# The second layer of a four-layer network: one matrix for each gate, chunks of 1024 columns in a fixed order

## The chip, the cores and the metric

The kernel runs on one core of a Trainium2 chip. The metric is the device time of one execution in microseconds (us); lower is better. The engines are named as in the profile: PE (TensorE, its weight loads apart as PEld), DVE (VectorE), ACT (ScalarE), POOL (GpSimd) and SP (SyncE, which here only issues DMAs). A "q" after a name (ACTq, SPq) is the engine's queue where it issues DMAs or waits.

## The reference

Four layers follow each other on a tensor of 8 images, 16 channels and 128 x 128 pixels in float32. Each adds its result to its input. The change is in the second (the code calls it layer 1), between a normalization over pairs of channels and the sum with the input:

```python
x = x + _L1_conv_ref(_gn(x), Wc, bc, W1, b1, W2, b2, W3, b3, W4, b4)

def _L1_conv_ref(x, Wc, bc, W1, b1, W2, b2, W3, b3, W4, b4):
    out1 = jnp.mean(x, axis=(2, 3), keepdims=True)
    out3 = jnp.max(x, axis=(2, 3), keepdims=True)
    out2 = conv1x1(x, Wc, bc)
    out4 = conv1x1(x, W1, b1)
    wh = conv1x1(out2 / (out1 + EPS), W2, b2)
    wh_weight = sigmoid(tanh(wh))
    gray = conv1x1(out4 / (out3 + EPS), W3, b3)
    gray_weight = sigmoid(tanh(gray))
    return conv1x1(x * (1.0 + wh_weight + gray_weight), W4, b4)
```

Each conv1x1 is a 16 x 16 matrix on the channels of a pixel plus a bias. Between the two convolutions of a gate there is only a factor for each image and channel, from the mean or the maximum of the image. The layers around it (an attention block on 3 x 3 windows, rational functions, splines) are not touched.

## The kernel before

The 8 images times 16 channels lie on the 128 partitions; a row holds the 16384 pixels of an image's channel. The layers run one after another. The first leaves its result in DRAM and the statistics of it in SBUF; the second reads it into a tile x (line 758), which stays in SBUF and is updated in place by the second and third layer.

The weights of the second layer are loaded at the very start of the kernel (lines 218 to 226). Each of the five 16 x 16 matrices becomes a block diagonal 128 x 128 tile w1s[n], by a memset on POOL and eight DMAs issued by ACT (line 224), each followed by eight small DMAs that repeat a bias (rep, line 172). Other DMAs of ACT stand before and behind these. ACT takes its instructions in order, so its first activation, the square root of the first normalization (line 197, recorded as line 152), comes behind these issues. SP loads the input (line 240) at the same time, and DVE takes its statistics.

The second layer itself begins with weight work for the third and fourth layer: SP loads parts of the weights, DVE spreads them (line 784, 36 operations), multiplies and sums splines (lines 810, 812, 820, 814, 823). This work has no place written out; the scheduler lays it among the rest. Then come the normalization's mean and rs (group_stats, lines 178 to 206, which ends in rs at line 203), and rmean and rmax, the reciprocals of mean and maximum for each image and channel (lines 833 to 839).

Then 32 chunks of 512 columns (line 841). For each chunk: DVE normalizes x to y (line 844); for each of the two gates PE multiplies with w1s[n] (line 848), DVE adds the bias and multiplies with rmean or rmax (line 850), PE multiplies with w1s[2 + n] (line 852), ACT takes tanh with the bias and then the sigmoid (lut, line 152). DVE adds the two gates and 1 (line 857), POOL multiplies y with that (line 860), PE multiplies with w1s[4] (line 862), DVE adds bias and x (line 863) and takes the statistics of the new x for the next normalization (line 866). The order of the chunks on each engine is left to the scheduler. SBUF tiles of this loop have three buffers, PSUM tiles (p1, p2, p3 of one bank each) two.

The third layer begins when the statistics are complete: group_stats again, then POOL clears eight tiles f (line 909), and DVE, ACT and POOL make powers of x (lines 890 to 901) that go to DRAM and come back before its first product on PE (line 927).

An order is forced where in_turn is used (lines 210 to 215): it ties an instruction behind the one named before it in the same chain, without a wait, so that the scheduler keeps that order on the engine. The first, third and fourth layer use it; the second doesn't. The lut helper ties activations to the table set they need.

Of the kernel before, what the change touches and what calls it, by code (L numbers as in the profile page):

```python
# [9 lines left out]
F32 = mybir.dt.float32  # L10
AF = mybir.ActivationFunctionType
ALU = mybir.AluOpType
AX = mybir.AxisListType
PSUM = bass.MemoryType.PSUM
# [86 lines left out]
def kernel(  # L101
# [43 lines left out]
    def lut(out_, in_, func, **kw):  # L145
        name = sets.get(func, str(func))
        last = phase["all"]
        if name != phase["name"]:
            phase.update(name=name, first=None, all=[])
            if name == "exp_ln":  # L150
                begin(nc.scalar.preload_act_table_set("natural_log_exp_and_others").ins, last)
        ins = nc.scalar.activation(out_, in_, func, **kw).ins  # L152
        if phase["first"] is None:
            begin(ins, last)
        else:
            tc.add_manual_dep(ins, phase["first"].name, order, reason="table set")
        phase["all"].append(ins)
        return ins
# [51 lines left out]
    def in_turn(engine, ins):  # L210

        if engine in chain:
            tc.add_manual_dep(ins, chain[engine].name, order, reason="in turn")
        chain[engine] = ins
        return ins
# [3 lines left out]
    for n in range(5):  # L219
        t = cpool.tile([BC, BC], F32, name=f"w1_{n}")  # L220
        nc.gpsimd.memset(t, 0.0)
        for b in range(B):
            r = slice(b * C, (b + 1) * C)
            nc.scalar.dma_start(t[r, r], w1[n])
        w1s.append(t)
        b1s.append(rep(b1[n], B, f"b1_{n}"))

# [6 lines left out]
    with ExitStack() as l0:  # L234
# [137 lines left out]
        class Variances:  # L372
# [3 lines left out]
            def __init__(self, first, others):  # L376
                self.due = [first + n * others for n in (4, 2, 4, 2)]
                self.begun = [False] * 4

            def add(self, t, c, sq):  # L380
                i = t // 32
                self.due[i] -= 1
                pe(
                    banks[t : t + 32, 0],
                    halfvar[:, 30 - c : 62 - c],
                    sq,
                    start=not self.begun[i],
                    stop=self.due[i] == 0,
                )
                self.begun[i] = True  # L390
# [373 lines left out]
    with ExitStack() as l1:  # L764
        wp = l1.enter_context(tc.tile_pool(name="w1", bufs=1))
        tmp = l1.enter_context(tc.tile_pool(name="tmp1", bufs=3))

        wa = rational.tile([128, 2, 9, 4, C], F32, name="wa")
        wb = rational.tile([128, 2, 9, 4, C], F32, name="wb")
        chan = k_("chan").unsqueeze(2).to_broadcast([128, 4, C])
        for t, src, least in ((wa, a2, 0), (wb, q2, 1)):
            for s in range(2):
                dense = wp.tile([128, 144], F32, name="dense", bufs=2)
                nc.gpsimd.memset(dense, 0.0)
                for u in range(4):
                    for i in range(1, src.shape[0] // C + least):  # L780
                        lo, r = 32 * (u ^ s) + 4 * (i - 1), C * (i - least) + 4 * u
                        nc.sync.dma_start(dense[lo : lo + 4], src[r : r + 4])
                for n in range(9):
                    nc.vector.tensor_tensor(
                        t[:, s, n],
                        dense[:, n * C : (n + 1) * C].unsqueeze(1).to_broadcast([128, 4, C]),
                        chan,
                        ALU.mult,
                    )
        for s in range(2):  # L790
            for u in range(4):
# [12 lines left out]
        nc.sync.dma_start(w, w3_spline)  # L804
        sc = wp.tile([128, 144, 9], F32, name="sc")
        bs = wp.tile([BC, 144, 9], F32, name="bs")
        for i in range(8):
            nc.sync.dma_start(sc[i * C : (i + 1) * C], w3_scaler)
            nc.scalar.dma_start(bs[i * C : (i + 1) * C], w3_base)
        nc.vector.tensor_mul(w, w, sc)  # L810
        red = wp.tile([128, 9, C], F32, name="red")
        nc.vector.tensor_reduce(red.rearrange("p n f -> p (n f)"), w, AX.X, ALU.add)
        redb = wp.tile([BC, 9, C], F32, name="redb")
        nc.vector.tensor_reduce(redb.rearrange("p n f -> p (n f)"), bs, AX.X, ALU.add)
        for s in range(4):
            for p in range(2):
                if 0 <= s - p < 3:
                    n = slice(3 * (s - p), 3 * (s - p) + 3)

                    nc.vector.tensor_scalar_mul(wspl[:, s, :, p, :], red[:, n], -1.0 / 6.0)  # L820
                    rows = slice(32 * s, 32 * s + 32)
                    for g in range(2):
                        nc.vector.tensor_scalar_mul(
                            wbase[rows, g, :, p, :],
                            redb[rows, n],
                            k_("image")[rows, 2 * s + g : 2 * s + g + 1],
                        )

        mean, dm, rs, _ = group_stats(bn1, "1")
        xmax = wp.tile([BC, 1], F32, name="xmax")  # L830
        nc.vector.tensor_reduce(xmax, top, AX.X, ALU.max)

        rmean = wp.tile([BC, 1], F32, name="rmean")
        nc.vector.tensor_scalar(rmean, dm, rs, EPS, ALU.mult, ALU.add)
        nc.vector.reciprocal(rmean, rmean)
        rmax = wp.tile([BC, 1], F32, name="rmax")
        nc.vector.tensor_scalar(rmax, xmax, mean, rs, ALU.subtract, ALU.mult)
        nc.vector.tensor_scalar_add(rmax, rmax, EPS)
        nc.vector.reciprocal(rmax, rmax)
        ps = l1.enter_context(tc.tile_pool(name="ps1", bufs=2, space=PSUM))  # L840
        for j in range(NCH):
            cols = bass.ts(j, 512)
            y = tmp.tile([BC, 512], F32, name="y1")
            nc.vector.tensor_scalar(y, x[:, cols], mean, rs, ALU.subtract, ALU.mult)
            gates = []
            for n, r in ((0, rmean), (1, rmax)):
                p1 = ps.tile([BC, 512], F32, name="p1")
                mm(p1, w1s[n], y, start=True, stop=True)
                t1 = tmp.tile([BC, 512], F32, name="t1")
                nc.vector.tensor_scalar(t1, p1, b1s[n], r, ALU.add, ALU.mult)  # L850
                p2 = ps.tile([BC, 512], F32, name="p2")
                mm(p2, w1s[2 + n], t1, start=True, stop=True)
                gt = tmp.tile([BC, 512], F32, name=f"gate{n}")
                lut(gt, p2, AF.Tanh, bias=b1s[2 + n])
                lut(gt, gt, AF.Sigmoid)
                gates.append(gt)
            nc.vector.scalar_tensor_tensor(
                gates[0], gates[0], 1.0, gates[1], op0=ALU.add, op1=ALU.add
            )
            nc.gpsimd.tensor_mul(y, y, gates[0])  # L860
            p3 = ps.tile([BC, 512], F32, name="p3")
            mm(p3, w1s[4], y, start=True, stop=True)
            nc.vector.scalar_tensor_tensor(
                x[:, cols], p3, b1s[4], x[:, cols], op0=ALU.add, op1=ALU.add
            )
            nc.vector.bn_stats(bn2[:, j], x[:, cols])


    bn3 = cpool.tile([BC, NCH, 6], F32, name="bn3")
    with ExitStack() as l2:  # L870
# [51 lines left out]
        def product(p, w, g, k, n, q):  # L922

            dh, dw = divmod(n, 3)
            for u in range(4):
                lo = 32 * (u ^ (q % 2))
                yield mm(  # L927
                    p[64 * (u % 2) : 64 * (u % 2) + 64, u // 2],
                    w[lo : lo + 32, q % 2, n].rearrange("p c f -> p (c f)"),
                    fs[g * NP + q][lo : lo + 32, 4 * k + dh : 4 * k + dh + 4, dw : dw + W],  # L930
                    start=True,
                    stop=True,
                ).ins
# [488 lines left out]
```

## Time and profile before

| What | us |
|---|---|
| median of 3 runs (lowest to highest) | 11350.83 (11344.36 to 11351.51) |
| the profiled execution, whole | 11347.98 |
| its span in the profile | 11345.9 |
| the second layer's first product on PE starts (line 848) | 3431.5 |
| its last product ends (line 862) | 3627.1 |
| the third layer's first product starts (line 927) | 3659.3 |
| the fourth layer's first activation (line 1105) | 10667.3 |

The span begins with the first instruction of the profile and ends with its last; the execution's time is 2.1 us longer. The second layer has less than 2% of the span; the third has more than 60%. In the lists of groups, a line gives the source line, engine, operation, what is written from what, the number of instructions, then after the bar the busy time in us and the mean of one in ns, and after the second bar the idle time of the engine just before these instructions, with what ended it.

### The profile page before, as it was taken

The numbers are of one execution on the slowest core, as the hardware profiler recorded it, in microseconds if no ns is written. First come the engines' busy times: TensorE is split into PE (matmuls) and PEld (weight loads), VectorE is DVE, ScalarE is ACT, GpSimd is POOL, SyncE is SP. The second block draws the span as 40 slices with busy tenths as digits, with TensorE's granted clock in tenths as the row PEclk, the third lists the DMA queues.
The fourth block names the chain that finished last, engine by engine and source line by source line (L and its number), as shares of the span: only waits on it lengthen the run. The fifth ranks groups of instructions, "written<-read, shape, count | busy, mean of one in ns | idle before, by whom it ended". The sixth has DMA issues, their size and how long they took to land.

```text
span 11345.9 us, 174363 instructions
## 1 busy us (share of the span) xinstructions
PE 8924.7 (79%) x72492; PEld 2115.6 (19%) x72492; DVE 9125.6 (80%) x6935; ACT 8792.4 (77%) x7187; POOL 4870.3 (43%) x2697
## 2 busy tenths in 40 slices
PE   5999999999986777777777777777777777777788
PEld 1222222222222111111111111111111111111122
DVE  3555555555555699999999999999999999999865
ACT  2555555555543699999999999999999999999876
POOL 3556555565542743333333334343343334344300
PEclk8999999999998799999999999999999999999999
DMA  1000000000002300000000000000000000000022
GB/s 48 12 15 15 15 12 13 15 15 14 13 6 67 130 20 7 7 13 7 7 13 7 7 13 7 7 13 7 7 10 10 7 7 13 7 7 7 20 53 50
DMA packets 185552, 203.94 MB, mean 18 GB/s; under 512 B 42936, under 2 KB 151608, under 8 KB 182712
## 3 DMA queue, kind: packets, MB, share of 16 engines
q1 hardware_dynamic: 180264, 190.81, 6.3%
q8 instruction: 570, 9.34, 0.3%
q10 hardware_dynamic: 4496, 1.97, 0.1%
q14 instruction: 222, 1.82, 0.1%
HBM read 107.15 MB, written 60.04 MB: 15 GB/s over the span
## 4 chain that ended last, share of the span: by engine, by line
DVE 44%; PE 31%; ACT 14%; issue 5%; POOL 2%; DMA 1%; SPq 1%; DVEq 0%; ACTq 0%; POOLq 0%
DVE t L959 22%; PE banks L360 17%; DVE u L965 14%; PE pn L927 10%; ACT t L948 8%; DVE y L518 2%; PE acc L1278 2%; POOL y L527 1%; DVE x L538 1%; ACT u L152 1%; PE pd L927 1%; ACT hid L152 1%; SPq L1242 1%; DMA yd<-y 1%; DVE x L630 1%
## 5 line engine op out<-in xcount | busy, mean ns | idle before, releaser
L927 PE MATMUL pn<-f,wa 32*64 32x512 f32 x18432 | 3424.1, 626 | 1706.7 <-DVE u L965 1672.7
L980 POOL TENSOR_TENSOR v<-t,u 128x1024 f32<-128x1024 f32 x1152 | 2738.0, 2377 | 4027.0 <-DVE t L959 3865.8
L965 DVE TENSOR_TENSOR u<-pn,u 128x1024 f32<-128x1024 f32 x2304 | 2715.3, 1220 | 123.6 <-DVE t L959 6.9
L927 PE MATMUL pd<-f,wb 32*64 32x512 f32 x18432 | 2608.4, 628 | 158.4 <-ACT t L948 92.3
L959 DVE SCALAR_TENSOR_TENSOR t<-t,u 128x2048 f32<-128x2048 f32 x1152 | 2631.2, 2284 | 34.4 <-ACT u L152 33.9
L948 ACT ACTIVATE t<-pd 128x1024 f32<-128x1024 f32 x2304 | 2336.7, 1014 | 320.0 <-PE pn L927 312.6
L152 ACT ACTIVATE u<-t 128x2048 f32<-128x2048 f32 x1152 | 2202.5, 1912 | 54.8 <-PE acc L1011 19.1
L152 ACT ACTIVATE u<-u 128x2048 f32<-128x2048 f32 x1152 | 2190.9, 1902 | 0.0
L927 PEld LDWEIGHTS pn<-f,wa 32*64 32x64 f32 x18432 | 752.0, 132 | 3777.2 <-DVE u L965 3243.1
L972 DVE SCALAR_TENSOR_TENSOR u<-t,u 128x1024 f32<-128x1024 f32 x1152 | 1419.1, 1232 | 37.6
L152 ACT ACTIVATE hid<-banks 128x1024 f32<-128x1024 f32 x576 | 571.4, 1023 | 1044.4 <-PE banks L360 1042.6
L1011 PE MATMUL acc<-u,const 128*32 128x512 f32 x9216 | 1263.2, 621 | 1.9 <-DVE u L972 1.9
L527 POOL TENSOR_TENSOR y<-y 128x1536 f32<-128x1536 f32 x256 | 894.6, 3495 | 830.5 <-DVE y L518 830.5
L518 DVE TENSOR_TENSOR y<-banks,vp 128x1536 f32<-128x1536 f32 x384 | 673.2, 1753 | 274.6 <-PE banks L360 271.3
L544 ACT ACTIVATE sq<-x 128x1024 f32<-128x1024 f32 x384 | 397.9, 1054 | 413.4 <-DVE x L538 290.7
L470 POOL TENSOR_TENSOR pd<-q,kp 128x1536 f32<-128x1536 f32 (+1 forms) x256 | 693.4, 2733 | 6.8 <-PE banks L360 6.7
L927 PEld LDWEIGHTS pd<-f,wb 32*64 32x64 f32 x18432 | 515.3, 132 | 753.3 <-ACT t L948 691.0
L360 PE MATMUL banks<-att,const 32*128 32x512 f32 x2304 | 497.4, 668 | 173.9 <-DVE att L509 96.2
L360 PE MATMUL banks<-h,wfc 64*128 64x512 f32 (+1 forms) x3072 | 619.7, 632 | 14.5 <-DVE h L606 14.5
L1011 PE MATMUL acc<-v,const 128*32 128x512 f32 x4608 | 616.8, 606 | 0.2 <-POOL v L980 0.2
L606 DVE TENSOR_TENSOR h<-banks,x 128x1024 f32<-128x1024 f32 x192 | 232.6, 1211 | 435.5 <-ACT hid L152 227.5
L1278 PE MATMUL acc<-s,wspl 128*32 128x512 f32 x3072 | 386.8, 646 | 92.6 <-DVE o L1291 92.6
(177 smaller groups left out, 7501.1 us busy)
## 6 DMA issues: line engine op xcount, KB each, us to landing
f<-yd SPq DMA_DIRECT2D x512, 101.6 KB
yd<-y SPq DMA_DIRECT2D x320, 130.0 KB
xin<-in_x SPq DMA_DIRECT2D x752, 32.0 KB
four<-sil SPq DMA_DIRECT2D x256, 65.0 KB
xj<-in_x SPq DMA_DIRECT2D x8, 1024.0 KB
xl<-in_x SPq DMA_DIRECT2D x32, 256.0 KB
x1d<-xl SPq DMA_DIRECT2D x32, 256.0 KB
x<-x1d SPq DMA_DIRECT2D x8, 1024.0 KB
```

Of the source, the lines that this page charges most:

```text
L152: ins = nc.scalar.activation(out_, in_, func, **kw).ins
L360: in_turn("pe", mm(*args, skip_group_check=True, **kw).ins)
L470: ins = nc.gpsimd.tensor_mul(t[:, :n].rearrange("p n (a b) -> p n a b", a=4), rows(self.q[d][:, k]).unsqueeze(1).to_broadcast([128, n, 4, W]),
L518: ins = nc.vector.tensor_mul(y.rearrange("p n (a b) -> p n a b", a=4), banks[:, 1:4].rearrange("p n (a b) -> p n a b", a=4), windows(v, j, 3),
L527: in_turn("pool", nc.gpsimd.tensor_add(self.y[k], self.y[k], y).ins)
L927: yield mm(p[64 * (u % 2) : 64 * (u % 2) + 64, u // 2], w[lo : lo + 32, q % 2, n].rearrange("p c f -> p (c f)"), fs[g * NP + q][lo : lo + ...
L948: in_turn("act", nc.scalar.activation(self.t[:, ab], self.pd.pop(ab), AF.Abs).ins)
L959: ins = nc.vector.scalar_tensor_tensor(self.t, self.t, 1.0, self.u, op0=ALU.add, op1=ALU.mult).ins
L965: ins = nc.vector.tensor_mul(self.u[:, ab], self.pn.pop(ab), self.u[:, ab]).ins
L972: ins = nc.vector.scalar_tensor_tensor(r, self.t[:, :, 0], 2.0, r, op0=ALU.subtract, op1=ALU.mult).ins
L980: ins = nc.gpsimd.tensor_mul(self.v, self.t[:, :, 1], self.u[:, :, 1]).ins
L1011: ins = mm(accs[k][32 * q : 32 * q + 32], gather[:, int(part == 1), g], (c.u[:, ab, 0], c.u[:, ab, 1], c.v[:, ab])[part], start=first, sto ...
```

## The change

The two convolutions of a gate are made one. With the factor r of the image between them, W2 (r (W1 y + b1)) + b2 is (W2 r W1) y + (W2 r b1 + b2). So after rmean and rmax are known, the kernel scales w1s[2 + n] by r, multiplies the two matrices and the bias on PE, and copies the results to SBUF: a 128 x 128 matrix gates[n] and a column shifts[n] for each gate. For this product the first matrix of each gate is needed the other way round, so line 224 loads w1[0] and w1[1] transposed, by an access pattern on the DRAM side.

The loop then has 16 chunks of 1024 columns. A chunk is an object with steps; each step's instructions on DVE, PE and ACT are put into a chain of that engine with in_turn. One sigmoid covers both gates. Each turn of the loop works on three chunks: the gates of chunk j, the norm of chunk j + 1, the sum of the gates and POOL's multiplication of chunk j - 1, and the last product and update of chunk j - 2. In PSUM the gate products have three buffers of two banks and the last product one of two banks, which is all of it. In SBUF y has five buffers and the gates three. The products of the setup have a PSUM pool of their own that is closed before.

```diff
-            nc.scalar.dma_start(t[r, r], w1[n])
+            nc.scalar.dma_start(t[r, r], w1[n].rearrange("i o -> o i") if n < 2 else w1[n])
...
-        ps = l1.enter_context(tc.tile_pool(name="ps1", bufs=2, space=PSUM))
-        for j in range(NCH):
-            cols = bass.ts(j, 512)
-            y = tmp.tile([BC, 512], F32, name="y1")
-            nc.vector.tensor_scalar(y, x[:, cols], mean, rs, ALU.subtract, ALU.mult)
-            gates = []
+
+        gates, shifts = [], []
+        with tc.tile_pool(name="ps_gate", bufs=2, space=PSUM) as pp:
             for n, r in ((0, rmean), (1, rmax)):
-                p1 = ps.tile([BC, 512], F32, name="p1")
-                mm(p1, w1s[n], y, start=True, stop=True)
-                t1 = tmp.tile([BC, 512], F32, name="t1")
-                nc.vector.tensor_scalar(t1, p1, b1s[n], r, ALU.add, ALU.mult)
...
+                scaled = wp.tile([BC, BC], F32, name=f"scaled{n}")
+                nc.vector.tensor_scalar_mul(scaled, w1s[2 + n], r)
+                pg = pp.tile([BC, BC], F32, name="pg")
+                mm(pg, w1s[n], scaled, start=True, stop=True)
+                ph = pp.tile([BC, 1], F32, name="ph")
+                mm(ph, scaled, b1s[n], start=True, stop=True)
+                gate = wp.tile([BC, BC], F32, name=f"w_gate{n}")
+                nc.vector.tensor_copy(gate, pg)
+                shift = wp.tile([BC, 1], F32, name=f"b_gate{n}")
+                nc.vector.tensor_add(shift, ph, b1s[2 + n])
+                gates.append(gate)
+                shifts.append(shift)
+        ps = l1.enter_context(tc.tile_pool(name="ps1", bufs=3, space=PSUM))
+
+        class Chunk:
+            def __init__(self, j):
+                self.j, self.x = j, x[:, bass.ts(j, 1024)]
+
+            def norm(self):
+                self.y = tmp.tile([BC, 1024], F32, name="y1", bufs=5)
+                ins = nc.vector.tensor_scalar(
+                    self.y, self.x, mean, rs, ALU.subtract, ALU.mult
+                ).ins
+                in_turn("dve1", ins)
+
+            def product(self, p, w):
+                for i in range(2):
+                    cols = bass.ts(i, 512)
+                    in_turn("pe1", mm(p[:, cols], w, self.y[:, cols], start=True, stop=True).ins)
+
+            def gate(self):
+                self.g = tmp.tile([BC, 2, 1024], F32, name="gate")
+                for n in range(2):
+                    p = ps.tile([BC, 1024], F32, name="p_gate")
+                    self.product(p, gates[n])
+                    in_turn("act1", lut(self.g[:, n], p, AF.Tanh, bias=shifts[n]))
+                in_turn("act1", lut(self.g, self.g, AF.Sigmoid))
+
+            def add(self):
+                g = self.g
+                ins = nc.vector.scalar_tensor_tensor(
+                    g[:, 0], g[:, 0], 1.0, g[:, 1], op0=ALU.add, op1=ALU.add
+                ).ins
+                in_turn("dve1", ins)
+                nc.gpsimd.tensor_mul(self.y, self.y, g[:, 0])
+
+            def last(self):
+                self.p = ps.tile([BC, 1024], F32, name="p_last", bufs=1)
+                self.product(self.p, w1s[4])
+
+            def update(self):
+                ins = nc.vector.scalar_tensor_tensor(
+                    self.x, self.p, b1s[4], self.x, op0=ALU.add, op1=ALU.add
+                ).ins
+                in_turn("dve1", ins)
+                for i in range(2):
+                    j = 2 * self.j + i
+                    ins = nc.vector.bn_stats(bn2[:, j], self.x[:, bass.ts(i, 512)]).ins
+                    in_turn("dve1", ins)
+
+        chunks = [Chunk(j) for j in range(HW // 1024)]
+        chunks[0].norm()
+        for j in range(len(chunks) + 2):
+            steps = (("gate", j), ("norm", j + 1), ("add", j - 1), ("last", j - 2), ("update", j - 2))
+            for do, i in steps:
+                if 0 <= i < len(chunks):
+                    getattr(chunks[i], do)()
```

More of the change, by code (lines that the diff above doesn't have):

```diff
@@ L839 @@
         nc.vector.reciprocal(rmax, rmax)
-        ps = l1.enter_context(tc.tile_pool(name="ps1", bufs=2, space=PSUM))
-        for j in range(NCH):
-            cols = bass.ts(j, 512)
-            y = tmp.tile([BC, 512], F32, name="y1")
-            nc.vector.tensor_scalar(y, x[:, cols], mean, rs, ALU.subtract, ALU.mult)
-            gates = []
-            for n, r in ((0, rmean), (1, rmax)):
-                p1 = ps.tile([BC, 512], F32, name="p1")
-                mm(p1, w1s[n], y, start=True, stop=True)
-                t1 = tmp.tile([BC, 512], F32, name="t1")
[L850 to L866, printed above, removed]
```

## The prediction

> **What bounds the kernel now.** I read the page first: which engine is full, and where.
>
> ```profile
> PE 8924.7 (79%) x72492; PEld 2115.6 (19%) x72492; DVE 9125.6 (80%) x6935; ACT 8792.4 (77%) x7187; POOL 4870.3 (43%) x2697
> ```
>
> No engine is full on average, and the average says nothing of the second layer, 198 us of 11346. So the next view is busy time by window: the whole second layer, ten of its chunks in the steady state, and the start of the kernel, which one line of the diff touches.
>
> ```profile
> 3431.00:3629.00 198.00, 154.13 (x320) 60.22 (x320) 136.70 (x239) 84.87 (x131) 43.75 (x37) 0.96 0.07 21
> 3545.00:3601.00 56.00, 45.74 (x102) 18.22 (x101) 39.55 (x61) 25.38 (x41) 12.65 (x10) 1.00 0.00 0
> 0.00:59.00 59.00, 1.17 (x4) 1.00 (x4) 22.00 (x40) 0.35 (x1) 3.83 (x20) 1.00 0.51 161
> ```
>
> The columns are length, then PE, PEld, DVE, ACT and POOL busy, clock, DMA share, GB/s. In the steady state PE is busy 82% and DVE 71%; neither is full, so the order of work leaves holes. Third view: the groups of those 56 us.
>
> ```profile
> L848 PE MATMUL p<-y,w 128*128 128x512 f32 x42 | 19.8, 592 | 0.0
> L852 PE MATMUL p<-t,w 128*128 128x512 f32 x40 | 18.8, 592 | 0.0
> L152 ACT ACTIVATE gate<-p,b 128x512 f32<-128x512 f32 x21 | 14.2, 678 | 30.0 <-PE p L852 30.0
> L860 POOL TENSOR_TENSOR y<-y,gate 128x512 f32<-128x512 f32 x10 | 12.7, 1265 | 43.2 <-DVE gate L857 43.2
> L152 ACT ACTIVATE gate<-gate 128x512 f32<-128x512 f32 x20 | 12.6, 629 | 0.6
> L862 PE MATMUL p<-y,w 128*128 128x512 f32 x20 | 11.3, 644 | 10.3 <-DVE t L850 10.3
> L850 DVE TENSOR_SCALAR t<-p,b,rmax 128x512 f32<-128x512 f32 x10 | 8.1, 805 | 0.0
> L850 DVE TENSOR_SCALAR t<-p,b,rmean 128x512 f32<-128x512 f32 x10 | 8.0, 802 | 0.0
> L857 DVE SCALAR_TENSOR_TENSOR gate<-gate,gate 128x512 f32<-128x512 f32 x11 | 7.6, 692 | 4.8 <-ACT gate L152 4.8
> L863 DVE SCALAR_TENSOR_TENSOR x<-p,b,x 128x512 f32<-128x512 f32 x10 | 7.5, 750 | 12.1 <-PE p L862 12.1
> L866 DVE BATCH_NORM_STATS2 bn<-x 128x6 f32<-128x512 f32 x10 | 6.9, 686 | 0.0
> L844 DVE TENSOR_SCALAR y<-x,mean,rs 128x512 f32<-128x512 f32 x10 | 5.4, 537 | 0.0
> ```
>
> Each f32 product of 512 columns is two MATMUL records. PE waits 10.3 us in ten chunks, for DVE's L850. Fourth view, the chain of waits over one chunk:
>
> ```profile
> 3584.50 1.46 DVE t L850 x2
> 3585.95 0.04 issue
> 3585.99 1.12 PE p L862 x2
> 3587.11 0.87 PE p L852 x2
> 3587.99 0.02 issue
> 3588.01 0.70 ACT gate L152
> ```
>
> It repeats every 5.58 us (L862 starts at 3585.99 and 3591.57). The path passes from PE to ACT to DVE and back; no engine carries it alone. Fifth, the timeline of the start:
>
> ```profile
> 54.88 3.73 ACTq L172 DMA_DIRECT2D b<-in_b  x8
> 58.65 1.28 ACT L152 ACT_TABLE_LOAD   x1 [58.65 <-DMA b<-in_b]
> 60.18 0.16 DVE L199 RECIPROCAL s<-s 128x1 f32<-128x1 f32 x1 [13.72 <-ACT s L152]
> ```
>
> ACT issues DMAs one after another, about 0.47 us apart, until 58.65; only then can it take the square root for which DVE waits 13.7 us. Whatever the changed L224 adds to ACT's queue is added to the end.
>
> **What the Trainium skill says.** "TensorE: Matmul & The Clock Gate", section Part 1: after an idle window of about 3.4 us the array runs at half clock until a busy window has passed. The trace agrees: MATMULs start 0.86 us apart from 3431.5 to about 3437, then 0.43 us. "ScalarE: Activation LUTs", section What ACT_TABLE_LOAD costs: 186 ns plus 0.833 ns an element, a pointer operand 93 ns more. The 629 ns without a bias agree (estimate 612), the 678 with one nearly (705). "SBUF — State Buffer", section Who interferes with whom: DVE's fast tensor_scalar and a GpSimd operation exclude each other. The trace agrees: an L844 issued beside L860 took 1083 ns, not 537, and ended 0.29 us after it. "DMA: Bandwidth & Descriptors", section Rules for kernel authors: a strided last dimension becomes one descriptor per element. No row here shows a DMA of that kind of any size.
>
> **The change part by part.** Sums are against the profiled execution's own 11347.98 us.
>
> *1. Steady state.* PE: L848 and L852 fall from four products per 512 columns to two; L862 stays. That is 12 MATMULs per 1024 columns at 0.4285 us (1.71 us for four in a row, from the timeline), 5.14 us, against 2 x 5.58 = 11.16 now.
> Do the others fit into 5.14? ACT: two tanh of 1024 from PSUM with a bias (678 + 512 x 0.833 = 1.10 us each) and one sigmoid of 2048 (row L152 u<-u, 1.90): 4.1. DVE, each 0.08 less from start to start as the timeline shows: the norm 0.81 (L1110, 128x1024, 0.69, plus 0.12 by which L844 exceeds its 512 form, for two pointers), the sum 1.23 (L972), the update 1.29 (L863 plus 512 columns at 1.04 ns), two bn_stats 1.37; 4.3 in all, as both L850 are gone. POOL: 2.37 (L980, 128x1024). So PE is the bound, if the order lets it run.
> The order: with PE's iteration j starting at 0, the gates of j end at 3.6, tanh at 4.8, sigmoid at 6.6. DVE meanwhile does the update of j-2 (after PE's last product, 5.35 to 6.6), statistics to 7.8, norm to 8.5, sum of j to 9.7; POOL to 12.2. PE wants this at 10.28 + 3.43 = 13.7: 1.5 us to spare. Around that loop (product 1.9, update 1.2, statistics 1.2, norm 0.7, sum 1.3, multiplication 2.55) go 8.9 us in two periods of 5.14. Fits.
>
> *2. Setup of the two matrices.* It comes after rmean and rmax and before the first product: scale 0.3, two small product pairs at half clock 1.5 (L184: MATMUL 0.35 and weight load 0.31 each), copy and add 0.4, the second gate partly beside the first, and the new pool takes all eight banks, so it waits for the last copy. Nothing covers it: +3 us (1 to 5); the first gate product goes from 3431.5 to 3434.5.
>
> *3. Filling.* From that point, half clock for about 3 us: gates of chunk 0 to 5.1, table load 1.28, tanh to 7.1, second table load 8.4 (both are there before, at 3437.05 and 3439.62), sigmoid 10.2, sum 11.5, POOL 14.0, first last-product 15.8. PE has by then done the gates of chunks 1 and 2.
>
> *4. Then* 13 iterations of 5.14 = 66.8, to 82.6. *Draining:* the last gates end at 80.9; tanh, sigmoid to 84.1; DVE first ends the update and statistics of chunk 13, sum to 86.4, POOL 89.0, last product, cold again after 4.7 us idle (L862 took 2.07 there before), 92.5.
>
> *5. What lies between.* L784 x36 (0.22 each), L810, L812 (1.5 each) and L820 are 12 us of DVE work in the layer. Before, L810 and L812 cost PE some 8 us around 3523 to 3540. DVE has 0.8 us spare per iteration, and 1.3 us of L784 fit into the slack of 1.5: I take +1.5, and +1 for a clock below 1.00 (0.96 over the layer now). Bounds: 0, and +12 if DVE meets one of them before its DMA has landed.
>
> The last product ends at 3434.5 + 92.5 + 2.5 = 3529.5; now at 3627.1. Gain 97.6. After it comes the same tail: POOL's f memsets (9.2 us) wait for the last product and cover the longer update and statistics of a 1024 chunk (2.5 us plus 4.4 for the group statistics, under 9.5).
>
> *6. The transposed loads.* 16 DMAs of L224 get 256 runs of 4 bytes, not 16 runs of 64. Before: 0.43 us to issue. Below: no change (the 128-run rows L903 and L1242 issue in 0.54 and 0.60). Above: in proportion to L1242, 1.2 us, +12 us. The moving itself: "VectorE: DVE Perf Modes", The three transpose paths, puts a strided copy of 128x128 at 19 times 1309 ns; estimate 1.5 ns an element, 0.4 us for 256. The x loads have 12 us of cover (variance ready at 46.5, root at 58.65); the issue has none. I take +2.
>
> Sum: -97.6 + 2 = -95.6, 11252 for the profiled execution. The median is 2.85 higher: 11255.
>
> **The rivals.** *A, PE is not the bound:* POOL or DVE is slower beside the other, the loop of 8.9 us grows past 10.3. For it: 1.5 us of slack is little, and the 1083 ns. Against: in the order given, norm and multiplication don't meet. A period of 6.0 adds 13 x 0.86 = 11: 11266. *B, the loads cost more:* 3 us each instead of 0.47, +40 less the 2 counted: 11293. *C, slower:* the transposed loads hold ACT's queue, each until it has landed element by element; from 0.47 + 97.6/16 = 6.6 us each the whole gain is gone; at 8 us, 120 lost, 11373. For it: ACT's root stands behind them uncovered, and "DMA b<-in_b" appears in that wait. Against: 128 runs take no longer than 48 (L284, 0.57). *D, the three chunks don't overlap:* gates 3.6, tanh 1.1, sigmoid 1.9, sum 1.2, POOL 2.4, product 1.9, 0.6 between: 12.7 x 16 = 203 against 195.6, some 11360, slower too; the order written out speaks against it.
>
> **How the numbers follow.** Forecast 0.74, A 0.10, B 0.08, C 0.05, D 0.01, better than the range 0.02. Low end: nothing for part 5 (-2.5) or 6 (-2), setup 1 (-2), and up to 9 if some of the f memsets move ahead of the last product: some 11239. High end: +10 for part 6, +12 for a late DMA in part 5, +7 of A: 11284. Within 0.2% (23 us, about what a measurement can tell) only a share of B and C lies: 0.02. Slower 0.06, faster 0.92.
>
> **What would show it.** Right: MATMULs 0.43 us apart through the layer, 12 per 5.14 us; PE busy near 100% there; a layer of about 98 us; ACT's root at 59 to 62. Wrong: PE idle before the last product of each chunk behind POOL (A); long ACTq rows at L224 (B, C); tanh of a chunk only after the update of the one before (D); DVE idle before L784 or L810 on a DMA.

## The result, and the profile after

| What | before | after |
|---|---|---|
| median of 5 runs each (lowest to highest), us | 11348.92 (11344.36 to 11351.51) | 11249.29 (11242.48 to 11250.59) |
| the profiled execution, whole | 11347.98 | 11250.13 |
| its span | 11345.9 | 11248.3 |

The kernel after takes 0.9911 of the time before, with a 95% interval of 0.9898 to 0.9925: about 99.6 us faster. The forecast was 11255, in a range of 11239 to 11284.

Cut into stages, the two profiles compare as follows. Every mark is the start or end of one instruction in the timeline; "rs" is the end of line 203 in the second layer's group_stats.

| Stage, us | before | after | difference |
|---|---|---|---|
| start to ACT's table load for the first root | 58.65 | 62.40 | +3.75 |
| from there to rs | 3371.70 | 3376.27 | +4.57 |
| rs to the second layer's first gate product | 1.16 | 3.95 | +2.79 |
| that product to the end of the last product | 195.64 | 95.56 | -100.08 |
| from there to the third layer's first product | 32.16 | 32.14 | -0.02 |
| from there to the end | 7686.58 | 7678.02 | -8.56 |

First the layer itself. These are groups of instructions of after, between its first and last product (busy us and mean ns after the first bar, idle time before them after the second):

```profile
L872 PE MATMUL p_gate<-y,w_gate 128*128 128x512 f32 x128 | 59.1, 607 | 3.6 <-DVE y L864 2.2 <-ACT gate L152 1.0 <-issue 0.4
L888 POOL TENSOR_TENSOR y<-y,gate 128x1024 f32<-128x1024 f32 x16 | 40.0, 2502 | 72.5 <-DVE gate L884 40.5 <-DMA dense<-in_a 31.9
L152 ACT ACTIVATE gate<-p_gate,b_gate 128x1024 f32<-128x1024 f32 x32 | 35.3, 1113 | 16.2 <-PE p_gate L872 15.3 <-POOL y L888 0.7
L872 PE MATMUL p_last<-y,w 128*128 128x512 f32 x64 | 30.9, 605 | 5.9 <-POOL y L888 2.8 <-DVE bn L901 2.7 <-DVE x L895 0.4
L152 ACT ACTIVATE gate<-gate 128x2048 f32<-128x2048 f32 x16 | 30.6, 1911 | 0.5
...
L864 DVE TENSOR_SCALAR y<-x,mean,rs 128x1024 f32<-128x1024 f32 x13 | 10.4, 799 | 0.0
```

PE had 320 MATMULs here and now has 192 (128 + 64). Its idle time in the whole layer is 3.6 + 5.9 us. Before, it was 41.1 us ahead of the last products. The group of them in before, and three lines of one of its chunks:

```profile
L862 PE MATMUL p<-y,w 128*128 128x512 f32 x64 | 38.6, 687 | 41.1 <-DVE t L850 26.9 <-POOL y L860 14.2
```

```profile
3476.87 0.81 DVE L850 TENSOR_SCALAR t<-p,b,rmax 128x512 f32<-128x512 f32 x1
3477.12 1.26 POOL L860 TENSOR_TENSOR y<-y,gate 128x512 f32<-128x512 f32 x1 [4.32 <-DVE gate L857]
...
3478.44 1.13 PE L862 MATMUL p<-y,w 128*128 128x512 f32 x2 [1.71 <-POOL y L860]
```

The name L850 in the first of these lines misleads, and the prediction took it over. L862 reads y, which POOL's L860 writes, and in each of the 32 chunks it starts 0.05 us after L860 has ended. In 23 of them an L850 happens to end within 0.04 us of L860, and the profile names that one. In the other nine, as in the chunk shown, L850 was done at least 0.4 us before PE's wait ended, and PE waited all the same; this chunk comes 5.58 us after the one ahead of it, like those where the two ends coincide. So PE waited for POOL's multiplication. That L850 is gone does not by itself end this wait; the experiments below tell what does.

ACT does as many elements in fewer and longer instructions. The stretch without filling and draining shows the same by engine (length, then PE, PEld, DVE, ACT, POOL busy, clock):

```profile
3458.00:3530.00 72.00, 69.23 (x159) 29.18 (x157) 67.12 (x110) 55.38 (x41) 33.87 (x16) 1.00 0.10 20
```

PE is busy 96% of it (82% before). DVE is at 93%, close behind; this matters below. One period, in the timeline (start and length in us, engine, line, what; in brackets the idle time before it and what ended it):

```profile
3504.07 0.80 DVE L864 TENSOR_SCALAR y<-x,mean,rs 128x1024 f32<-128x1024 f32 x1
...
3504.78 1.88 PE L872 MATMUL p_last<-y,w 128*128 128x512 f32 x4
...
3504.78 1.22 DVE L884 SCALAR_TENSOR_TENSOR gate<-gate 128x1024 f32<-128x1024 f32 x1
...
3506.17 2.37 POOL L888 TENSOR_TENSOR y<-y,gate 128x1024 f32<-128x1024 f32 x1 [2.78 <-DVE gate L884]
...
3506.49 3.60 PE L872 MATMUL p_gate<-y,w_gate 128*128 128x512 f32 x8
3506.69 1.28 DVE L895 SCALAR_TENSOR_TENSOR x<-p_last,b,x 128x1024 f32<-128x1024 f32 x1 [0.70 <-PE p_last L872]
...
3509.93 1.88 PE L872 MATMUL p_last<-y,w 128*128 128x512 f32 x4
```

Last products start 5.15 us apart. No PE line has a wait in brackets. POOL's multiplication ends at 3506.17 + 2.37 = 3508.54, and PE takes its result at 3509.93: 1.4 us of slack, where the forecast had 1.5. DVE's norm (L864) is over before POOL begins.

PE still waits once for long. Weight work of the later layers stands in DVE's queue before the norm of a chunk:

```profile
3518.19 2.01 DVE L810 TENSOR_TENSOR w<-w,sc 128x1296 f32<-128x1296 f32 x1
...
3523.38 0.80 DVE L864 TENSOR_SCALAR y<-x,mean,rs 128x1024 f32<-128x1024 f32 x1
...
3524.33 1.96 PE L872 MATMUL p_gate<-y,w_gate 128*128 128x512 f32 x4 [2.22 <-DVE y L864]
```

Between L810 and L864 stand L812, L820 and the statistics; the 2.22 us in brackets are PE's wait.

### The profile page after: what moved, and what is told of

It reads as the page before. It is cut to its first block, busy times and chain, and to the rows that moved or that the text cites. A ratio compares the mean times of both kernels' runs of the same rounds, so it can differ in the third digit from the quotient of the medians.

```text
span 11248.3 us, 173864 instructions
## 1 busy us (share of the span) xinstructions
PE 8843.7 (79%) x72372; PEld 2092.2 (19%) x72372; DVE 9068.7 (81%) x6829; ACT 8780.2 (78%) x7107; POOL 4873.1 (43%) x2681
## 3 DMA queue, kind: packets, MB, share of 16 engines
q10 hardware_dynamic: 8336, 1.97, 0.1%
## 4 chain that ended last, share of the span: by engine, by line
DVE 44%; PE 31%; ACT 14%; issue 5%; POOL 2%; DMA 1%; SPq 1%; DVEq 0%; ACTq 0%; POOLq 0%
DVE t L1003 22%; PE banks L360 17%; DVE u L1009 14%; PE pn L971 10%; ACT t L992 9%; DVE y L518 2%; PE acc L1322 2%; ACT u L152 1%; POOL y L527 1%; DVE x L538 1%; ACT hid L152 1%; PE pd L971 1%; DMA yd<-y 1%; DVE x L630 1%; SPq L1286 1%
## 5 line engine op out<-in xcount | busy, mean ns | idle before, releaser
L1322 PE MATMUL acc<-s,wspl 128*32 128x512 f32 x3072 | 389.2, 650 | 92.5 <-DVE o L1335 92.5
```

## The experiments

Twelve runs were made, two of them of the kernels of the study once more. Each comparison is with before in the same session, whose median was between 11343.77 and 11351.89. Their stages, from one profile each (in us, as in the table above; "last bn1 to rs" is from the start of the first layer's last bn_stats to rs):

| Kernel | root at | root to rs | last bn1 to rs | layer | tail | third layer to end |
|---|---|---|---|---|---|---|
| before | 58.65 | 3371.70 | 15.53 | 195.64 | 32.16 | 7686.58 |
| before_again | 58.44 | 3372.65 | 15.17 | 195.63 | 32.18 | 7686.87 |
| after | 62.40 | 3376.27 | 15.55 | 95.56 | 32.14 | 7678.02 |
| after_again | 61.66 | 3373.00 | 15.93 | 97.94 | 31.83 | 7679.46 |
| plain_loads | 58.19 | 3368.31 | 15.38 | 95.65 | 31.98 | 7681.16 |
| all_transposed | 66.02 | 3367.79 | 15.63 | 95.98 | 31.52 | 7678.09 |
| merge_only | 62.06 | 3372.95 | 15.29 | 138.85 | 30.61 | 7681.28 |
| order_only | 61.49 | 3373.83 | 15.16 | 148.20 | 31.43 | 7683.30 |
| chunks_512 | 60.27 | 3371.30 | 15.87 | 98.50 | 31.34 | 7676.06 |
| one_by_one | 63.34 | 3376.39 | 15.64 | 109.01 | 31.45 | 7681.55 |
| weights_split | 63.08 | 3362.37 | 6.19 | 125.01 | 31.68 | 7685.32 |
| f_early | 61.46 | 3363.26 | 5.47 | 103.15 | 30.11 | 7679.55 |
| best | 57.83 | 3358.28 | 5.47 | 126.55 | 30.32 | 7684.06 |
| best_late | 56.56 | 3356.97 | 5.47 | 96.41 | 29.40 | 7687.24 |

**The two kernels once more.** The table of stages has +4.57 and -8.56 in places that the change doesn't touch.

> The kernel after, unchanged, profiled once more. In the first pair of profiles the stretch from ACT's root to the second layer's rs was 4.6 us longer than before (8.33 in all, of which 3.75 at the root), and the stretch from the third layer's first product to the end 8.6 us shorter, with the same instructions in both. Theory: both come from the execution (when the TensorE clock falls and rises), so this profile differs from the first by several us in one or both of these stretches, and the second layer's first to last product stays at 95.6 within 0.5. Rival: the change itself moves them; then both stretches are within 1 us of the first profile of after.

> The kernel before, unchanged, profiled once more. Theory (the execution): rs at 3430.3 and third layer to end 7686.6 move by several us from their values in the first profile. Rival (the change): both stay within 1 us. The layer's first to last product stays at 195.6 within 0.5 either way.

Measured: 11249.62 and 11349.11 in one run each. From root to rs after went from 3376.27 to 3373.00, before from 3371.70 to 3372.65, and kernels with the same first layer lie between 3367.79 and 3376.39: this stretch varies from execution to execution, as the theory of after_again said. before moved by only 0.95 and 0.29, as the rival of before_again had it and not its theory; and that the clock is the reason was not shown. From the third layer to the end neither kernel moved by more than 1.5. The two profiles of before are above both of after; but best_late, which has the merged matrices too, took 7687.24. The instructions are the same, and in after each of the third layer's steps of about 429 us is some 0.5 us shorter. Its cause stays open. The layer of after missed its margin of 0.5: it took 97.94. The first products show a part of it, after above, after_again below:

```profile
3442.62 10.24 PE L872 MATMUL p_gate<-y,w_gate 128*128 128x512 f32 x20 [0.36 <-issue]
```

```profile
3438.61 11.75 PE L872 MATMUL p_gate<-y,w_gate 128*128 128x512 f32 x20 [0.36 <-issue]
```

The same 20 MATMULs took 1.5 us longer, and the last eight of the layer had 5.54 us busy at a granted clock of 0.83, where after had 3.97 at 1.00. So when the clock falls and rises differs between executions of the same kernel.

**What the transposed loads cost.** plain_loads has the first line, all_transposed the second, each with the host's arrays turned to match:

```diff
-            nc.scalar.dma_start(t[r, r], w1[n].rearrange("i o -> o i") if n < 2 else w1[n])
+            nc.scalar.dma_start(t[r, r], w1[n])
```

```diff
-            nc.scalar.dma_start(t[r, r], w1[n].rearrange("i o -> o i") if n < 2 else w1[n])
+            nc.scalar.dma_start(t[r, r], w1[n].rearrange("i o -> o i"))
```

> After, but w1_0 and w1_1 come from the host already in the orientation wanted and are loaded row by row, 16 runs of 64 bytes, as before. Theory (step 6, the transposed loads delay ACT's queue): ACT's table load for the first root goes back from 62.40 to 58.65, the time falls by 3.7 us (3 to 4.5). Rival (the 3.75 come from the queue's landing times and vary between executions): root within 1 us of 62.4, time the same.

> After, but all five matrices of the second layer are loaded transposed element by element, 24 more such DMAs, with the host giving the other three the other way round. Step 6 at +3.75 us for 16 of them (0.23 each) gives 24 x 0.23 = 5.6 us more: root at 68, time 11255. Rival B of the prediction (3 us each instead of 0.47) gives 60 us more; rival C (6.6 or more each) 147 or more. Third theory, the cost sits in the first groups behind the queue's depth only: under 2 us more.

Measured: 11243.86 (11241.03 to 11247.71; ratio to before 0.991, interval 0.9897 to 0.9924) and 11249.05 (11237.68 to 11254.13; 0.9914, 0.99 to 0.9927). The times scatter by more than these loads cost; the root's place in the profile tells it, 58.19 and 66.02 (58.65 and 68 were forecast). ACT's queue in after, then in all_transposed:

```profile
54.84 3.75 ACTq L224 DMA_DIRECT2D w<-in_w  x8
...
62.40 1.28 ACT L152 ACT_TABLE_LOAD   x1 [62.40 <-DMA b<-in_b]
```

```profile
57.69 4.33 ACTq L224 DMA_DIRECT2D w<-in_w  x8
...
66.02 1.28 ACT L152 ACT_TABLE_LOAD   x1 [66.02 <-DMA b<-in_b]
```

The root starts at 57.93 on the mean of the five profiles without a transposed load (56.56 to 58.65), at 61.97 on that of the eight with 16 (60.27 to 63.34), at 66.02 with 40: 4.04 / 16 = 0.25 us each for the first 16 and 4.05 / 24 = 0.17 for the others. The place at 66.02 is from one profile, so whether the two figures differ is open. The eight issues shown of all_transposed take 4.33 us, 0.54 each; the group that after shows here is a plain one, 0.47 each. That is the cheap end: while SP still loads the input, the second and third group of all_transposed take 7.91 and 8.18 us for eight, 5.64 and 5.85 in before. In after the two transposed groups take 5.06 and 5.98 (5.03 and 5.64 in before), and the small bias loads behind them got longer instead, 7.18 and 5.32 us for eight (6.01 and 3.91). Which issues of the queue take the added time is thus not the same each time. Rivals B (3 us) and C (6.6) are out by more than a factor of ten. That the loads move the root by some 4 us is shown; that the time falls by it is consistent with the medians and not resolved by them.

**Merging, order and chunk length apart.** merge_only is the loop of before on the merged matrices:

```diff
-                p1 = ps.tile([BC, 512], F32, name="p1")
-                mm(p1, w1s[n], y, start=True, stop=True)
-                t1 = tmp.tile([BC, 512], F32, name="t1")
-                nc.vector.tensor_scalar(t1, p1, b1s[n], r, ALU.add, ALU.mult)
-                mm(p2, w1s[2 + n], t1, start=True, stop=True)
+                mm(p2, gates[n], y, start=True, stop=True)
-                lut(gt, p2, AF.Tanh, bias=b1s[2 + n])
+                lut(gt, p2, AF.Tanh, bias=shifts[n])
```

order_only keeps the loop of after, without merging; the second products of the gates are a step of their own, behind the last product of chunk j - 2. It loads w1_0 and w1_1 in the orientation of after, so its first products apply other weights than the reference; the instructions and their shapes are those wanted.

```diff
-                    self.product(p, gates[n])
-                    in_turn("act1", lut(self.g[:, n], p, AF.Tanh, bias=shifts[n]))
+                    self.product(p, w1s[n], self.y)
+                    ins = nc.vector.tensor_scalar(t1, p, b1s[n], r, ALU.add, ALU.mult).ins
+                    in_turn("dve1", ins)
...
+                    self.product(p, w1s[2 + n], self.ts[n])
+                    in_turn("act1", lut(self.g[:, n], p, AF.Tanh, bias=b1s[2 + n]))
```

chunks_512 is after with 512 for 1024 and one product and one bn_stats instead of two. one_by_one is after without in_turn in the layer:

```diff
-        for j in range(len(chunks) + 2):
-            steps = (("gate", j), ("norm", j + 1), ("add", j - 1), ("last", j - 2), ("update", j - 2))
+        for c in chunks:
+            for do in ("norm", "gate", "add", "last", "update"):
+                getattr(c, do)()
```

> The loop of before (chunks of 512, the compiler's order, one chunk written after the other) with the two matrices made one for each gate; no order by hand. Theory (as in the prediction's part 1 and rival D: PE's instructions alone don't set the time, the order does): per 512 columns the chain y, two gate products, tanh, sigmoid, sum, POOL, last product, update stays, only L850 and one pair of products leave it; the period falls from 5.58 to about 3.6, the layer from 195.6 to some 125, time 11279. Rival (the merging is nearly all of it, PE then is the bound at 2.57 per 512): layer near 95, time 11249.

> Chunks of 1024 in a fixed order with three on their way, but the two convolutions of a gate kept (20 MATMULs instead of 12 per 1024, and both L850 on DVE), without the setup of the matrices. Theory: DVE then has 4.3 + 2 x 1.34 + 0.16 = 7.1, PE 20 x 0.4285 = 8.57; PE is the bound and gives 16 x 8.57 + about 25 of filling and draining = 162, time 11316: about a third of the gain. Rival (order and chunk size are most of the gain): layer under 125. Third: the additional waits of DVE between the two products break the order, layer over 185.

> After with chunks of 512 columns in the same fixed order (32 of them). Theory: PE needs 2.57 for each chunk, DVE 5 instructions of 2.67 in all with 0.4 saved by start to start, 2.35; ACT two tanh 0.68 and a sigmoid of 1024 1.05, 2.4; POOL 1.2. All fit by sum, but the loop of last product, update, statistics, norm, sum, multiplication for 512 columns, 0.87 + 0.75 + 0.69 + 0.54 + 0.69 + 1.2 + 0.4 = 5.1 against two periods 5.14, has no slack left: period 2.6 to 2.9 for 512, layer 92 to 100 (filling and draining are shorter by some 8). Rival (the long chunks carry the gain): layer over 120.

> After without the fixed order: chunks of 1024, merged matrices, each chunk written out whole after the one before, so the compiler orders the engines. Theory (the order by hand lets PE run ahead; rival D of the prediction is what its absence would give at worst, 12.7 per chunk): the compiler's own order overlaps about two chunks as it did before (5.58 against a chain of some 12 for 512 columns), layer 110 to 150, time 11265 to 11305. Rival (the order by hand adds nothing to chunk size and merging): layer within 3 us of 95.6.

| Kernel | us (lowest to highest) | ratio to before, interval | layer | PE busy in it | PE idle in it |
|---|---|---|---|---|---|
| before | as above | 1 | 195.64 | 154.1 | 41.5 |
| merge_only | 11292.35 (11288.18 to 11299.25) | 0.9953, 0.9938 to 0.9968 | 138.85 | 101.4 | 37.4 |
| order_only | 11300.05 (11298.39 to 11301.70) | 0.9959, 0.9944 to 0.9974 | 148.20 | 143.0 | 5.3 |
| after | 11249.29 (11242.48 to 11250.59) | 0.9911, 0.9898 to 0.9925 | 95.56 | 86.4 | 9.2 |
| chunks_512 | 11247.40 (11242.75 to 11253.18) | 0.9913, 0.9898 to 0.9928 | 98.50 | 88.4 | 10.1 |
| one_by_one | 11257.02 (11250.54 to 11267.55) | 0.9919, 0.9903 to 0.9936 | 109.01 | 91.1 | 18.0 |

Merging alone takes 57 us from the layer, the new loop (order, longer chunks, more buffers, one sigmoid for both gates) alone 47, both 100. The last two columns tell what each part does. Merging takes work from PE: 128 MATMULs at 0.4285 us are 54.8 us, and its busy time falls by 52.7; its waiting hardly changes. The loop takes the waiting, 41.5 to 5.3 us, and leaves most of the work. merge_only took 14 us more than its theory had (125), but the rival (95) is out. In a window of 80 us of it no engine is full (PE 59.36, DVE 60.73 us busy). PE waits before each last product, as this group of that window shows:

```profile
L874 PE MATMUL p<-y,w 128*128 128x512 f32 x38 | 23.0, 688 | 16.3 <-POOL y L872 16.3
```

This is the wait for POOL that before has too. It goes only when PE has other products to do meanwhile, and the new loop gives it those: order_only has no PE wait for POOL between 3460 and 3560. order_only did better than forecast (162): PE is at its own limit there, 59.80 of 60 us busy; only filling and draining were put too high, 148.2 - 16 x 8.57 = 11 instead of 25.

chunks_512 gives the same time as after. Once the order is fixed, the length of 1024 is worth about 3 us of the layer, little more than the 2.4 between the two profiles of after. Without the order one_by_one (1024) needs 30 us less than merge_only (512), and between merge_only and chunks_512, both with 512, lie 40. Neither of these two differences is one thing alone: merge_only also has the buffers of before and two sigmoids for each chunk, and no run separates these from the length or the order. Between one_by_one and after only the order differs: 13 us. What one_by_one lacks against after shows in its timeline:

```profile
3500.79 2.37 POOL L886 TENSOR_TENSOR y<-y,gate 128x1024 f32<-128x1024 f32 x1 [3.65 <-DVE gate L883]
...
3501.74 1.96 DVE L864 TENSOR_SCALAR y<-x,mean,rs 128x1024 f32<-128x1024 f32 x1
```

The norm stands beside POOL's multiplication, takes 1.96 us instead of 0.80 and ends 0.54 us after it; the mean over eleven is 1472 ns, against 799 in after. DVE is then busy 68.26 of 70 us, twelve chunks in that time, and sets the pace at 5.8 us a chunk. This is the exclusion between a fast tensor_scalar of DVE and an operation of GpSimd of which "SBUF — State Buffer" of the Trainium skill, section Who interferes with whom, speaks, and the trace agrees. The order by hand puts the norm just ahead of the multiplication, where it costs nothing.

**The weight work of DVE.** weights_split cuts L810, L812 and L814 into thirds by columns and puts one piece into DVE's fixed order in each iteration:

```diff
+            if j > 2:
+                ins = next(pieces, None)
+                if ins is not None:
+                    in_turn("dve1", ins)
```

> After, but the work on the later layers' weights (L810, L812, the reduction behind it) is cut into thirds along the columns, and one piece of it at a time stands in DVE's fixed order of the second layer, after the statistics of each chunk from the fourth on. Theory (part 5 of the prediction: the whole pieces of 1.5 to 2.0 us, two or three in a row, exceed DVE's slack and hold PE for about 2.5 us once): no PE wait over 0.7 us between the filling and the draining, layer 95.56 (97.94 in the second profile) less 2 to 2.5: 93 to 95.5. Rival (the pieces cost their 5 us wherever they stand, since DVE is near its limit too): layer 96 or more. In the time, 2 us is below what it can tell.

Measured: 11271.79 (11269.82 to 11277.00; ratio 0.9931, 0.9918 to 0.9945), layer 125.01, 29 us longer than in after. The theory is out; the rival's "96 or more" holds as a number, but its reason, pieces of 5 us in all, doesn't explain 29. DVE's timeline:

```profile
3480.00 0.61 DVE L816 TENSOR_TENSOR w<-w,sc 128x432 f32<-128x432 f32 x1 [11.89 <-DMA sc<-in_w_scaler]
```

The first piece stood in the order before its data had landed (three groups of L784 before it had waited 5.39, 4.05 and 4.36 us for theirs). Together with these DVE waited 25.7 us, and what stands behind such an instruction on its engine waits with it: PE had no product for 29.98 us, until a norm behind that piece was done at 3481.34. Its clock had meanwhile fallen to 0.50. The stretch ahead of the layer got 9.4 us shorter (last bn1 to rs 6.19 instead of 15.55), for the reason that f_early shows below. This is the upper bound that the forecast gave to its part 5 ("+12 if DVE meets one of them before its DMA has landed"), and more than twice as large.

**The filling of f.** f_early takes the eight tiles f from the pool "rational" and fills them before the loop:

```diff
+        fs = [rational.tile([128, 10, WP], F32, name=f"f{i}") for i in range(2 * NP)]
+        for t in fs:
+            nc.gpsimd.memset(t, 1.0)
         wa = rational.tile([128, 2, 9, 4, C], F32, name="wa")
```

> After, but the eight tiles f of the third layer are allocated and filled with ones before the second layer's loop, so POOL has nothing to fill after the last product. Theory (as the prediction has it, POOL's 9.2 us of filling cover the update, statistics and group statistics after the last product and end some 2 us after these): from last product's end to the third layer's first product 29.5 to 30.5 instead of 31.8 to 32.1. Rival (the path there is the chain of statistics and the stores and loads behind it, the fill is covered): within 0.3 of 32. Third: the fills collide with POOL's first multiplications or DVE's setup and lengthen the layer or its start by more than they save.

Measured: 11246.78 (11243.28 to 11248.39; ratio 0.9908, 0.9895 to 0.9922). The tail is 30.11, as the theory had it, against 31.43 to 32.14 in the other kernels with chunks of 1024 that fill f behind the loop. But two other stages moved by more: last bn1 to rs went from 15.55 to 5.47 us, and the layer from 95.56 to 103.15. Both have one cause, a place in DVE's queue. In after:

```profile
3428.89 0.16 DVE L199 RECIPROCAL s<-s 128x1 f32<-128x1 f32 x1 [1.37 <-ACT s L152]
3434.33 1.50 DVE L814 TENSOR_REDUCE redb<-bs 128x144 f32<-128x1296 f32 x1 [5.28 <-DMA bs<-in_w_base]
...
3435.88 2.42 DVE L823 TENSOR_SCALAR wbase<-redb,const 32x48 f32<-32x48 f32 x12
...
3438.51 0.16 DVE L203 RECIPROCAL rs<-s 128x1 f32<-128x1 f32 x1
```

The scheduler put L814 and L823, which the fourth layer needs, into the middle of the chain to rs. DVE waits 5.28 us for bs and works 3.9 more while the whole second layer waits for rs. It is so in before too (15.53 us), hence no part of the difference. In f_early they fell behind rs, where DVE waited 10.94 us for bs during the filling. The third theory came true in part too: some of the fills stand between the first layer's last operations on POOL, and DVE waits there 4.89 us for POOL, 2.71 in after.

**All together.** best has plain loads, f_early and the thirds of weights_split.

> After with the three together: plain row loads of w1_0 and w1_1, weight work in thirds in DVE's fixed order, f filled before the loop. If each does by itself what its theory says: root 3.6 us earlier, layer 2 to 2.5 shorter, tail 2 shorter, 7 to 8.5 us in all, time 11241 (11249 median of after). If the parts are hidden or covered: within 2 us of plain_loads, 11244.

Measured: 11268.28 (11262.78 to 11275.64; 0.9929, 0.9915 to 0.9942); both expectations missed it by over 20 us; the early pieces outweigh the rest, layer 126.55. So best_late takes all the weight work, cuts it smaller, gives the tile dense four buffers instead of two, and places the pieces by the time at which their data are there:

```diff
+            room += 0.85 if 4 <= j < 16 else 4.0 if j == 16 else 0.0
+            while room > 0.1:
+                cost, ins = next(pieces, (room, None))
+                if ins is not None:
+                    in_turn("dve1", ins)
+                room -= cost
```

> After with plain row loads of w1_0 and w1_1, f filled before the loop, and all of the weight work on DVE (L784, L810, L812, L814, L820, L823) taken out of the compiler's hands: cut into pieces of 0.14 to 0.55 us that stand in DVE's fixed order after the statistics of the chunks, 0.85 us of them for each iteration from the fifth on, each piece 5 us or more after its DMA is due, the rest in the draining. Theory: in both kernels of the study DVE meets L814 inside the chain to rs and waits 5.3 us for the load of bs, 9.4 us in all with L823 behind it; in weights_split it met L810's load too early and PE lost 30 us. With neither, last statistics of the first layer to rs takes 5.5 instead of 15.5, the layer 93 to 97, the tail 30, the root is 3.6 earlier: 9.4 + 3.6 + 2 + 0 to 2 = 15 to 17 us, time 11232 to 11234 by the medians of after (11249.3). Rival (the weight work comes back as waits of PE in the loop, as in weights_split and best): layer over 105, time 11243 or more.

Measured: 11236.33 (11232.33 to 11239.96), ratio 0.9905, interval 0.9889 to 0.9922. Its stages are those expected: last bn1 to rs 5.47, layer 96.41, tail 29.40, and no wait of DVE for a weight. PE is busy without a gap from 3440 to 3500. The median is 13 us below that of after and 2 to 4 above what was expected; in the profiled execution the third layer to the end took 9.2 us more than in after, for which no cause was found. Measured against before in each one's own session the gain grows from 99.6 to 107.4, by 8; the two intervals of the ratio overlap. That the version is the fastest of all is likely, by how much is not settled.

## Why the prediction was right, by its steps

One reading of it was wrong: the wait ahead of L862, which it put to DVE's L850, was for POOL's L860, and so the path of a chunk went from PE to ACT, to DVE's L857, to POOL and back. The sums did not rest on that name. They count PE's products and ask whether the other engines and the loop through POOL fit into 5.14 us in the order given, and that is what happened. The name would have misled a forecast of merging alone.

1. *Steady state* (PE the bound at 5.14): 5.15 measured, PE 96% busy, POOL with 1.4 us of slack for 1.5. Chunks of 512 with the same order, and a layer at PE's own limit in order_only, show that PE's products and the loop carry this, not the length of the chunks.
2. *Setup* (+3, 1 to 5): +2.79.
3. *Filling* (15.8 to the end of the first last product): 16.4, from 3442.62 to 3459.01.
4. *Thirteen iterations and draining* (92.5 in all): 95.56 less the stall of part 5; the layer was to take 95.0 with it, and took 95.56, and 97.94 in the second profile. There the clock takes more than the +1 counted: the first 20 MATMULs are 1.5 us longer than in after, and the last four take 3.56 us instead of 1.98.
5. *Weight work* (+1.5, 0 to +12): one wait of 2.22. (That L810 and L812 had cost PE some 8 us before is too much: L862 starts at 3518.94 and, three chunks later, at 3541.32, which is 5.6 us more than three times 5.58.) weights_split shows that the upper bound was real and too low: 29 us where the first piece comes before its data.
6. *Transposed loads* (+2, 0 to +12): +3.75 in the first pair, 4.0 between the means of all profiles; the term was mis-sized by 2. The cover of 12 us held, but the 0.4 us for the moving stretches its source, which speaks of a large stride on the destination's side; here the stride is on the source's, and no run times the moving by itself.

After the last product the tail is the same (32.16 and 32.14), and POOL's filling of f covers the longer update, as said; f_early takes 2 us away by moving it.

The terms that the sum didn't have are +4.57 in the first layer and -8.56 from the third layer on. They come to -4 together and more than make up for the 2 us by which the loads were underestimated. That the profiled execution, 11250.13, lies within 2.3 us of the forecast for it, 11252.4, is therefore in part luck; the parts inside the layer are not. The first of the two terms varies between executions; the second is open.

Of the rivals, A (DVE or POOL slower beside the other, a period of 6.0) is what one_by_one shows without the order, with 5.8, and didn't come true with it. B and C put 3 and over 6.6 us on each load; 0.17 to 0.25 more than before were measured. D (no overlap, 203) is further off than even the order that the scheduler finds by itself, 109.

## What to carry to other kernels

Separate the work of an engine from its waiting: merging two products took 57 us from the layer, nearly all of it work; a loop with other chunks' products ready during the wait took 40 more, and the chunk length 3 once that loop was there. Check the name that a profile gives to a wait against what the waiting instruction reads, above all where two engines end at the same moment. A fixed order has a price: an instruction in it whose data are late holds up all that follows, so work from outside is placed by the landing of its DMA, not by free time alone. And look through the short chain of scalars ahead of a layer for instructions that don't belong to it.

## What was not expected of the hardware

- An element-wise transposed load of 16 x 16 values added 0.17 to 0.25 us to the queue of ACT. Its issue takes 0.54 us against 0.47 when the input has landed, and about 1.0 against 0.7 in two groups while the input is being loaded (all_transposed against before). "DMA: Bandwidth & Descriptors" of the Trainium skill, section Rules for kernel authors, has one descriptor for each element; ACT's queue had 8336 packets instead of 4496, which is 16 times 240 more and agrees, but the issuing engine is held far less than in proportion to the 16 times as many descriptors.
- The same 20 products at the start of the layer took 10.24 us in one execution and 11.75 in another: with idle time ahead of it, PE's first microseconds are not the same each time. A single profile can't resolve 2 us in this layer.
